# Mamba block: decays per channel group in PSUM, one scan per group, input products on GpSimd, one projection buffer

## Chip, cores, metric

The kernel runs on one NeuronCore of one Trainium2 chip. The metric is device time in microseconds (us) of one execution; less is better. Before the change the median of three runs is 3686.44 us (3685.19 to 3687.99).

## What is computed

Four graph layers in sequence over 3327 nodes with 256 features each, padded to 26 tiles of 128 nodes; each adds its result to its input and normalizes. The change touches layer 1 alone: a graph convolution, then a Mamba block whose state-space recurrence runs over the nodes in order.

```python
h = relu(adj @ x @ gcn_w + gcn_b); h = layernorm(h)
xz = h @ w_in                        # 512 channels xc, 512 channels z
u = silu(conv(xc) + conv_b)          # causal, 4 taps
dbc = u @ w_xp                       # dt (16), B (16), C (16)
dt = softplus(dbc[:, :16] @ w_dt + b_dt)
dA = exp(dt[:, :, None] * A[None])   # (L, 512, 16)
dBu = dt[:, :, None] * B[:, None, :] * u[:, :, None]
def step(hst, inp):                  # over the L nodes
    dAt, dBut, Ct = inp
    hst = dAt * hst + dBut
    return hst, hst @ Ct
_, ys = lax.scan(step, zeros, (dA, dBu, C))
y = (ys + u * D_skip) * silu(z)
return y @ w_out
```

## The kernel before

**Tiling.** Channels lie on the partitions: 512 channels are four groups (`NG`) of 128. Nodes lie along the free dimension, in eight chunks whose ends grow: 128, 256, 384 and then five times 512 nodes (`WC`). A chunk has 16 states (`DS`), so there are 128 pairs of chunk and state, and the main loop (from line 551) goes through them in order.

**One state.** `row` (L453) fetches the rows B and C of this state by a DMA that spreads them over all partitions, two states ahead, into one of three buffers. `decay` (L460) makes exp(dt*A) on ScalarE, one activation for each channel group, into one of two SBUF buffers that hold all four groups side by side, each with one extra column in front. `feed` (L471) multiplies dt*u by the row of B on VectorE into one of three buffers `db`; the extra column receives the state carried over from the chunk before (the copy `du<-carry`, L469). `scan` (L478) is one VectorE scan over all four groups at once, 4 x 513 elements, since the extra column has decay 0 and so restarts the recurrence with the carried state. ScalarE then saves the last column of each group (`carry`, L486). The product with the row of C is a VectorE multiplication in place (L568), and `add_up` (L489) adds the result, transposed on TensorE, into up to four PSUM banks `y`.

**What runs between.** `head` (L363) prepares the next chunk in eleven pieces, one with each state from the fourth on: projections to PSUM (`ps`), three VectorE multiply-adds for each group (the convolution, L379), Silu, w_xp and w_dt products, softplus in steps (L407 to L420), and dt*u (L422). `gate_input` (L427) computes z; at L580 it goes through Silu. `gate` (L496), `gated`, `residual` and `back` finish the chunk before. `pump` (L326) advances `convolve` (L254), the adjacency product of layer 1, whose TensorE work is spread between the states. Its per-tile statistics go from VectorE to three very small GpSimd instructions (L251, L252, L296) and back to ScalarE. `values` prepares layer 2.

**Order and memory.** Each engine has one in-order queue; the order within it comes from the order of the program text and a scheduler that may move independent instructions, save where the text pins them. PSUM has eight banks of 128 x 512 f32: four `y`, three `ps` (every projection takes one), one `cb` for the adjacency product.

Of the kernel before, what the change touches and what calls it, by code (L numbers as in the profile page):

```python
# [18 lines left out]
P = 128  # L19
# [5 lines left out]
WC = 512  # L25
# [18 lines left out]
def gnn_kernel(ctx: ExitStack, tc: tile.TileContext, n: int, a: dict, out: bass.AP):  # L44
# [109 lines left out]
    with tc.tile_pool(name="l1b", bufs=1) as wpool, tc.tile_pool(name="l1at", bufs=2) as l1at:  # L154
# [33 lines left out]
        with tc.tile_pool(name="l1aw", bufs=1) as cwork, tc.tile_pool(name="l1c", bufs=2) as ch, \  # L188
                tc.tile_pool(name="l1t", bufs=3) as tmp, tc.tile_pool(name="l1s", bufs=2) as work, \
                tc.tile_pool(name="l1y", bufs=1, space=PSUM) as ypsum, \  # L190
                tc.tile_pool(name="l1p", bufs=3, space=PSUM) as psum, \
                tc.tile_pool(name="l1d", bufs=1, space=DRAM) as l1d, \
                tc.tile_pool(name="l1q", bufs=1, space=PSUM) as cpsum:
            def scratch():
# [50 lines left out]
            nch = len(ends)  # L245
            starts = [0] + ends[:-1]
            hTs, us, szs, rows_of = {}, {}, {}, {}

            def power(rs, var):

# [75 lines left out]
            def pump(steps=1, tiles=0):  # L326


                nonlocal done
                while steps > 0 or done < min(tiles, nt):  # L330
                    t = next(stream, None)
                    if t is None:
                        return values()
                    done, steps = t, steps - 1
# [28 lines left out]
            def head(c):  # L363
# [7 lines left out]
                for g in range(NG + 1):  # L371
                    if g < NG:
                        nc.scalar.copy(xc[:, g, 3:3 + w], project(c, g, w))
                        nc.scalar.activation(u[:, g, :], xc[:, g, 0:w], AF.Identity, scale=conv_w[:, g, 0:1],
                                             bias=conv_b[:, g:g + 1])
                    if g:
                        ug = u[:, g - 1, :]
                        for k in range(1, 4):
                            nc.vector.scalar_tensor_tensor(ug, xc[:, g - 1, k:k + w], conv_w[:, g - 1, k:k + 1], ug,  # L379
                                                           op0=ALU.mult, op1=ALU.add)  # L380
                    if g < NG:
                        yield None
                nc.gpsimd.tensor_copy(last, xc[:, :, w:w + 3])
                yield None
                nc.scalar.activation(u, u, AF.Silu)
                ps = psum.tile([P, WC], F32, name="ps")
                for g in range(NG):
                    nc.tensor.matmul(ps[:w_sp.shape[2], :w], w_sp[:, g, :], u[:, g, :],
# [10 lines left out]
                for g0 in range(0, NG, 2):  # L399
# [7 lines left out]
                        nc.scalar.activation(v[:, g, :], ps[:, :w], AF.Identity, bias=b_dt[:, g:g + 1])  # L407
                        nc.scalar.activation(e[:, g, :], ps[:, :w], AF.Abs, bias=b_dt[:, g:g + 1])
                    yield None
                nc.scalar.activation(e, e, AF.Exp, scale=-1.0)  # L410
                e1 = scratch()[:, :, :w]
                nc.scalar.activation(e1, e, AF.Identity, bias=1.0)
                yield None
                nc.vector.scalar_tensor_tensor(e, e1, 1.0, e, op0=ALU.subtract, op1=ALU.subtract)
                yield None
                nc.scalar.activation(e1, e1, AF.Ln)
                yield None
                nc.vector.tensor_sub(e1, e1, e)
                dt = ch.tile([P, NG, WC], F32, name="dt", bufs=1)[:, :, :w]
                nc.vector.scalar_tensor_tensor(dt, v, 0.0, e1, op0=ALU.max, op1=ALU.add)  # L420
                du = by_group(ch.tile([P, NG * (1 + WC)], F32, name="du", bufs=1), w)
                nc.vector.tensor_mul(du[:, :, 1:], dt, u)  # L422
                for g in range(NG):
                    nc.scalar.mul(u[:, g, :], u[:, g, :], d_skip[:, g:g + 1])
                yield c, dt, du
# [1 line left out]
            def gate_input(c, i):  # L427
# [5 lines left out]
                for k in range(2):  # L433
# [5 lines left out]

            dAs, dbs = ([cwork.tile([P, NG * (1 + WC)], F32, name=f"{x}{i}") for i in range(m)]
                        for x, m in (("dA", 2), ("db", 3)))

            def by_group(t, w):
                return t[:, :NG * (1 + w)].rearrange("p (g w) -> p g w", g=NG)


            lines = [cwork.tile([P, 2, 1 + WC], F32, name=f"row{i}") for i in range(3)]
            for r in lines:  # L450
                nc.vector.memset(r[:, 0, 0:1], 1.0)

            def row(c, s):  # L453

                w = us[c].shape[2]
                r = lines[(c * DS + s) % 3][:, :, :1 + w]
                nc.sync.dma_start(r[:, :, 1:], rows_of[c][None, :, s, :].to_broadcast([P, 2, w]))
                return r

            def decay(x, s):  # L460

                c, dt, du = x
                w = dt.shape[2]
                dA = by_group(dAs[s % 2], w)
                if s < 2 and (c == 0 or w != ends[c - 1] - starts[c - 1]):
                    nc.gpsimd.memset(dA[:, :, 0:1], 0.0)
                for g in range(NG):
                    nc.scalar.activation(dA[:, g, 1:], dt[:, g, :], AF.Exp, scale=A[:, g, s:s + 1])  # L468
                nc.scalar.copy(du[:, :, 0], carry[:, s, :])  # L469

            def feed(x, s, B):  # L471

                du = x[2]
                w = du.shape[2] - 1
                tc.keep_in_program_order(nc.vector.tensor_mul(  # L475
                    by_group(dbs[(x[0] * DS + s) % 3], w), du, B[:, 0:1, :].to_broadcast([P, NG, 1 + w])))

            def scan(x, s):  # L478

                w = x[1].shape[2]  # L480
                h = dbs[(x[0] * DS + s) % 3]
                m = NG * (1 + w)
                nc.vector.tensor_tensor_scan(h[:, :m], dAs[s % 2][:, :m], h[:, :m],  # L483
                                             initial=0.0, op0=ALU.mult, op1=ALU.add)
                h = by_group(h, w)
                nc.scalar.copy(carry[:, s, :], h[:, :, w])  # L486
                return h[:, :, 1:]

            def add_up(ys, h, first=False, last=False):  # L489

# [26 lines left out]
            def back(c):  # L517

                m = szs[c].shape[1]
                mv = small.tile([P, WC // P, 2], F32, name="mvc")  # L520
                ahead = gated(c, 0)
                for i in range(m):
                    gt, ahead = ahead, gated(c, i + 1) if i + 1 < m else None
                    residual(c, i, gt)
                    stats(mv[:, i, :], X[:, starts[c] // P + i, :])
                rs = small.tile([P, WC // P], F32, name="rsc")
                power(rs[:, :m], mv[:, :m, 1])
# [11 lines left out]
                yield  # L539

            pump(tiles=ends[0] // P)
            x = None
            for i, x in enumerate(head(0)):
                if i % 2:
                    pump()
            states = [(c, s) for c in range(nch) for s in range(DS)]
            rows = [row(*states[0]), row(*states[1])]
            decay(x, 0)
            feed(x, 0, rows[0])
            ys = ahead = None  # L550
            for c in range(nch):
                w = us[c].shape[2]
                for s in range(DS):
                    if s + 1 < DS:
                        nxt = (x, s + 1)
                    else:
                        nxt = (y, 0) if c + 1 < nch else None
                    k = c * DS + s + 2
                    if k < len(states):
                        rows.append(row(*states[k]))  # L560
                    if nxt:
                        decay(*nxt)
                    h = scan(x, s)
                    if s == 0 and c:
                        gate(c - 1, ys)
                    if nxt:
                        feed(*nxt, rows[1])
                    nc.vector.tensor_mul(h, h, rows.pop(0)[:, 1:2, 1:].to_broadcast([P, NG, w]))  # L568
                    if s == 0:
                        ys = [ypsum.tile([P, DI], F32, name=f"y{i}") for i in range(w // P)]  # L570
                        add_up(ys, us[c], first=True)
                    add_up(ys, h, last=(s == DS - 1))
                    if s == 0 and c:
                        tail = back(c - 1)
                    if s in (0, 4) and c:
                        next(tail)
                    if 2 <= s < 2 + w // P:
                        gate_input(c, s - 2)
                    if s == 8:
                        nc.scalar.activation(szs[c], szs[c], AF.Silu)  # L580
                    if c or s % 4 < 3:
                        pump()
                    if DS - 13 <= s < DS - 1 and c + 1 < nch:
                        if s == DS - 13:
                            pump(steps=0, tiles=ends[c + 1] // P)
                            ahead = head(c + 1)
                        y = next(ahead)
                if c + 1 < nch:
                    x = y
            gate(nch - 1, ys)  # L590

            m = us[nch - 1].shape[2] // P
            ahead = gated(nch - 1, 0)
            for i in range(m):
                it = starts[nch - 1] // P + i
                gt, ahead = ahead, gated(nch - 1, i + 1) if i + 1 < m else None
                residual(nch - 1, i, gt)
                mv = small.tile([P, 2], F32, name="mv")
                stats(mv, X[:, it, :])
                rs, nb = (small.tile([P, 1], F32, name=x) for x in ("rs", "nb"))  # L600
# [815 lines left out]
```

## Time and profile before

One execution was profiled: its own time is 3689.87 us, the profile's span 3688.1 us, the median of the runs 3686.44 us.

| stretch of the span (us) | what | length | TensorE busy | VectorE busy | ScalarE busy | GpSimd busy | granted clock |
|---|---|---|---|---|---|---|---|
| 0 to 394 | layer 0 and the start of layer 1 | 394 | 383.60 | 73.10 | 41.20 | 3.21 | 1.00 |
| 394 to 475 | chunk of 128 | 81 | 75.98 | 52.18 | 57.94 | 8.80 | 0.95 |
| 475 to 585 | chunk of 256 | 110 | 95.68 | 91.34 | 67.06 | 35.16 | 0.92 |
| 585 to 715 | chunk of 384 | 130 | 109.88 | 126.66 | 78.65 | 41.15 | 0.92 |
| 1541 to 1566 | end of layer 1 | 25 | 19.64 | 7.62 | 8.36 | 4.25 | 0.87 |
| 1566 to 3688 | layers 2 and 3 | 2122 | 2021.12 | 1432.73 | 1040.44 | 374.51 | 0.98 |

How to read it: busy is the time in which an engine worked on an instruction; the granted clock is TensorE's, as a share of full speed. The boundaries are the starts of each chunk's first scan. The four full chunks with a successor (715 to 1392) and the last one (to 1541) are shown with the prediction.

### The profile page before, as it was taken

To read this page: it belongs to the slowest core of one execution; us is meant where nothing else is said; L and a number is where in the kernel's file an instruction comes from. 1 tells how busy PE (TensorE), PEld (TensorE's weight loads), DVE (VectorE), ACT (ScalarE), POOL (GpSimd) and SP (SyncE) were. 2 spreads that over 40 slices of the span, in tenths; PEclk is the share of its full clock that TensorE was granted. 3 is DMA by queue.
4 is the path that set the end of the run, shared out by engine and by line. 5 is a ranking of instruction groups with operands and counts; after the bars stand their busy time and mean duration, and the time that the engine had idled before them with its cause. 6 is when DMAs were issued, how large, how long until landed. Compare 5 with 4: busy or idle time off the path is not lost. (4 is left out here: it accounts for less than half of the span.)

```text
span 3688.1 us, 42873 instructions
## 1 busy us (share of the span) xinstructions
PE 3277.3 (89%) x15583; PEld 2588.6 (70%) x15583; DVE 2577.8 (70%) x5207; ACT 1711.3 (46%) x2736; POOL 671.5 (18%) x850
## 2 busy tenths in 40 slices
PE   9999988887778656599989999999999899999996
PEld 7888766656556444488867777777777577777775
DVE  1111588999999999777754544544541999999996
ACT  1000665554546555211123333333334888888883
POOL 0000032343334100011110000000000233333332
PEclk9999999988888778699999999999999999999998
DMA  7443343332323121144422212112112222222220
GB/s 246 140 132 101 103 112 108 101 96 85 95 82 92 46 58 48 35 156 152 147 92 62 56 52 65 56 53 65 55 54 64 61 59 67 67 67 64 64 62 22
DMA packets 151993, 308.00 MB, mean 84 GB/s; under 512 B 19858, under 2 KB 73266, under 8 KB 151634
## 3 DMA queue, kind: packets, MB, share of 16 engines
q1 hardware_dynamic: 151762, 305.06, 27.8%
q8 instruction: 127, 2.08, 0.2%
q14 instruction: 104, 0.85, 0.1%
HBM read 294.36 MB, written 10.65 MB: 83 GB/s over the span
## 5 line engine op out<-in xcount | busy, mean ns | idle before, releaser
L483 DVE TENSOR_TENSOR_SCAN db<-dA,db 128x2052 f32<-128x2052 f32 (+3 forms) x128 | 464.1, 3626 | 0.7
L493 PE MATMUL y<-ident,db 128*128 128x128 f32 x1664 | 265.6, 323 | 142.6 <-DVE db L568 142.5
L493 PEld LDWEIGHTS y<-ident,db 128*128 128x128 f32 x1664 | 239.2, 170 | 186.9 <-DVE db L568 163.9
L892 PE MATMUL acc<-X,wt 128*128 128x256 f32 x1352 | 345.2, 392 | 10.5 <-ACT wt L890 10.2
L859 PE MATMUL acc<-F,at 128*128 128x256 f32 x1352 | 352.9, 386 | 1.0 <-ACT q L633 0.6
L892 PE MATMUL acc<-G,wt 128*128 128x256 f32 x1352 | 335.9, 391 | 5.8 <-ACT wt L823 5.5
L266 PE MATMUL cb<-F,at 128*128 128x256 f32 x1352 | 323.8, 392 | 9.4 <-ACT hn L287 8.1
L892 PEld LDWEIGHTS acc<-X,wt 128*128 128x128 f32 x1352 | 243.7, 190 | 105.7 <-issue 41.3
L116 PE MATMUL acc<-xa,at 128*128 128x257 f32 x1352 | 308.8, 381 | 5.9 <-DMA at<-in_adjT 5.8
L859 PE MATMUL acc<-X,at 128*128 128x256 f32 x1352 | 308.4, 381 | 0.0
L768 PE MATMUL acc<-F,at 128*128 128x257 f32 x1352 | 304.0, 381 | 0.7 <-ACT r L741 0.7
L904 DVE MAX8 cand<-e 128x8 f32<-128x128 f32 x676 | 142.3, 281 | 227.9 <-ACT e L845 216.3
L266 PEld LDWEIGHTS cb<-F,at 128*128 128x128 f32 x1352 | 260.4, 198 | 56.8 <-ACT hn L287 12.7
L468 ACT ACTIVATE dA<-dt,A_log 128x512 f32<-128x512 f32 (+3 forms) x512 | 294.3, 636 | 9.8 <-DVE dt L420 9.5
L892 PEld LDWEIGHTS acc<-G,wt 128*128 128x128 f32 x1352 | 250.1, 193 | 65.1 <-ACT wt L823 34.9
L859 PEld LDWEIGHTS acc<-F,at 128*128 128x128 f32 x1352 | 237.2, 190 | 75.0 <-issue 50.2
L116 PEld LDWEIGHTS acc<-xa,at 128*128 128x128 f32 x1352 | 255.3, 191 | 43.3 <-issue 6.6
L859 PEld LDWEIGHTS acc<-X,at 128*128 128x128 f32 x1352 | 252.8, 191 | 39.9 <-issue 7.8
L768 PEld LDWEIGHTS acc<-F,at 128*128 128x128 f32 x1352 | 253.7, 191 | 36.6 <-issue 1.0
L475 DVE TENSOR_TENSOR db<-du,row 128x2052 f32<-128x2052 f32 (+3 forms) x128 | 241.0, 1883 | 28.7 <-PE y L493 17.8
L568 DVE TENSOR_TENSOR db<-db,row 128x2048 f32<-128x2048 f32 (+3 forms) x128 | 241.5, 1887 | 26.6 <-ACT carry L486 26.6
L890 ACT COPY wt<-tp 128x512 f32<-128x512 f32 (+1 forms) x182 | 93.7, 557 | 311.0 <-PE tp L888 310.6
(307 smaller groups left out, 5382.0 us busy)
## 6 DMA issues: line engine op xcount, KB each, us to landing
at<-in_adjT SPq DMA_DIRECT2D x102, 832.0 KB, 4.5
at<-in_adjT SPq DMA_DIRECT2D x260, 320.0 KB, 3.0
row<-bc SPq DMA_DIRECT2D x80, 512.0 KB, 4.9
at<-in_adjT SPq DMA_DIRECT2D x52, 576.0 KB, 3.9
at<-in_adjT SPq DMA_DIRECT2D x26, 512.0 KB, 3.7
row<-bc SPq DMA_DIRECT2D x16, 384.0 KB, 5.0
row<-bc SPq DMA_DIRECT2D x16, 256.0 KB, 4.7
xt<-in_xT SPq DMA_DIRECT2D x26, 128.0 KB, 4.1
```

What stands on the lines that cost most here:

```text
L116: nc.tensor.matmul(acc, at[:, j, :], rhs[:, j0 + j, :], start=(j0 + j == 0), stop=(j0 + j == nt - 1))
L266: nc.tensor.matmul(acc, at[:, j % JC, :], X0[:, j, :], start=(j == 0), stop=(j == nt - 1))
L468: nc.scalar.activation(dA[:, g, 1:], dt[:, g, :], AF.Exp, scale=A[:, g, s:s + 1])
L475: tc.keep_in_program_order(nc.vector.tensor_mul(by_group(dbs[(x[0] * DS + s) % 3], w), du, B[:, 0:1, :].to_broadcast([P, NG, 1 + w])))
L483: nc.vector.tensor_tensor_scan(h[:, :m], dAs[s % 2][:, :m], h[:, :m], initial=0.0, op0=ALU.mult, op1=ALU.add)
L493: nc.tensor.matmul(y[:, g * P:(g + 1) * P], h[:, g, i * P:(i + 1) * P], ident, is_transpose=True, start=(first and g == 0), stop=(last and ...
L568: nc.vector.tensor_mul(h, h, rows.pop(0)[:, 1:2, 1:].to_broadcast([P, NG, w]))
L768: nc.tensor.matmul(acc, at[:, j, :], F[:, j0 + j, :], start=(j0 + j == 0), stop=(j0 + j == nt - 1))
L859: nc.tensor.matmul(acc, at[:, j, :], rhs[:, j0 + j, :], start=(j0 + j == 0), stop=(j0 + j == nt - 1))
L890: copy(wt[:, :m, :], pt[:, :m, :])
L892: nc.tensor.matmul(acc, wt[:, j, :], rhs[:, j0 + j, :], start=(j0 + j == 0), stop=(j0 + j == nt - 1))
L904: nc.vector.max(cand[:, s * 8:(s + 1) * 8], z[:, s * SEG:(s + 1) * SEG])
```

## The change

- **Decays in PSUM, one group each.** `decay(k, g)` writes exp(dt*A) of one group to a PSUM bank of its own, of which there are two (pool `l1a`). The two big SBUF buffers, the extra columns and the copy `du<-carry` go.
- **One scan per group.** Four scans of 512 instead of one of 2052; the carried state is the scan's `initial` operand, one value for each partition.
- **Input products on GpSimd.** `feed(k)` becomes a GpSimd multiplication of the same size, issued two states ahead, into two buffers `h` in place of three `db`. It waits for the product and the carry copy of state k-2, which read the same buffer.
- **Products** with the row of C go to two buffers of their own (`hc`).
- **One `ps` buffer** for all projections, where there were three; the banks are now four `y`, one `ps`, two `dA`, one `cb`.
- **Order.** `chained` pins the order of the scans, products and `head`'s VectorE instructions; `decaying` that of the decays, both Silu and Ln on ScalarE. `head`'s pieces are placed after the scans and ahead of the product; its Exp and the addition of 1 are issued by group. `gated` is no longer issued one tile ahead of `residual`. Silu of z moves from state 8 to state 7. `dt` gets a second buffer.

```diff
-                tc.tile_pool(name="l1p", bufs=3, space=PSUM) as psum, \
+                tc.tile_pool(name="l1p", bufs=1, space=PSUM) as psum, \
+                tc.tile_pool(name="l1a", bufs=2, space=PSUM) as apsum, \
...
+            def decaying(*x, **k):
+                with tc.issue_after(decays[-1].ins) if decays else nullcontext():
+                    decays.append(nc.scalar.activation(*x, **k))
+
+            def chained(op, *x, **k):
+                with tc.issue_after(chain[-1].ins) if chain else nullcontext():
+                    chain.append(op(*x, **k))
...
-                nc.scalar.activation(e, e, AF.Exp, scale=-1.0)
-                nc.scalar.activation(e1, e, AF.Identity, bias=1.0)
+                for g in range(NG):
+                    nc.scalar.activation(e[:, g, :], e[:, g, :], AF.Exp, scale=-1.0)
+                    nc.scalar.activation(e1[:, g, :], e[:, g, :], AF.Identity, bias=1.0)
...
-                for g in range(NG):
-                    nc.scalar.activation(dA[:, g, 1:], dt[:, g, :], AF.Exp, scale=A[:, g, s:s + 1])
-                nc.scalar.copy(du[:, :, 0], carry[:, s, :])
+                dA = apsum.tile([P, WC], F32, name="dA")[:, :w]
+                decaying(dA, dt[:, g, :], AF.Exp, scale=A[:, g, states[k][1]:states[k][1] + 1])
+                return dA
...
-                tc.keep_in_program_order(nc.vector.tensor_mul(
-                    by_group(dbs[(x[0] * DS + s) % 3], w), du, B[:, 0:1, :].to_broadcast([P, NG, 1 + w])))
+                nc.gpsimd.tensor_tensor(hs[k % 2][:, :, :w], du, rows[k][:, 0:1, :].to_broadcast([P, NG, w]), op=ALU.mult)
...
-                nc.vector.tensor_tensor_scan(h[:, :m], dAs[s % 2][:, :m], h[:, :m],
-                                             initial=0.0, op0=ALU.mult, op1=ALU.add)
+                h = hs[k % 2][:, g, :dA.shape[1]]
+                chained(nc.vector.tensor_tensor_scan, h, dA, h, initial=carry[:, s, g:g + 1] if c else 0.0,
+                        op0=ALU.mult, op1=ALU.add)
...
+            rows = {k: row(k) for k in range(2)}
+            for k in range(2):
+                feed(k)
+            dAs = [decay(0, g) for g in range(2)]
...
+                for g in range(NG):
+                    scan(k, g, dAs.pop(0))
+                    if g < 2:
+                        dAs.append(decay(k, g + 2))
+                    elif k + 1 < len(states):
+                        dAs.append(decay(k + 1, g - 2))
+                with tc.high_priority():
+                    nc.scalar.copy(carry[:, s, :], hs[k % 2][:, :, w - 1])
+                if s == 7:
+                    decaying(szs[c], szs[c], AF.Silu)
+                if DS - 13 <= s < DS - 1 and c + 1 < nch:
...
+                    xs[c + 1] = next(ahead)
+                h = product(k)
+                if k + 2 < len(states):
+                    feed(k + 2)
```

## The prediction

> **What bounds the kernel now.** The page first. Its chain of waits is no help: it ends after one instruction (ACT h L1138). So I read the costliest groups, cut the span at the first scan of each chunk, and asked for busy times in these stretches. Columns: length, then busy us (and instructions) of PE, PEld, DVE, ACT, POOL, then granted clock, DMA share, GB/s.
>
> ```profile
> 715.00:882.00 167.00, 134.45 (x640) 102.96 (x638) 162.45 (x85) 88.48 (x164) 64.70 (x19) 0.89 0.34 99
> 882.00:1056.00 174.00, 132.46 (x616) 102.55 (x616) 163.81 (x89) 88.58 (x165) 62.38 (x19) 0.85 0.31 89
> 1056.00:1228.00 172.00, 123.80 (x564) 94.96 (x564) 163.77 (x89) 88.53 (x165) 54.63 (x19) 0.84 0.28 76
> 1228.00:1392.00 164.00, 100.79 (x444) 76.62 (x445) 159.70 (x80) 90.41 (x192) 15.03 (x7) 0.76 0.19 51
> 1392.00:1541.00 149.00, 79.88 (x380) 65.02 (x379) 144.45 (x64) 61.61 (x143) 7.68 (x4) 0.75 0.19 48
> ```
>
> In the five full chunks VectorE is busy for 94 to 97%; nothing else is above 81%. The stage is bound by VectorE. The groups by shape say by what (count, busy us, mean ns):
>
> ```profile
> L483 DVE TENSOR_TENSOR_SCAN db<-dA,db 128x2052 f32<-128x2052 f32 x80 | 354.0, 4426 | 0.0
> L568 DVE TENSOR_TENSOR db<-db,row 128x2048 f32<-128x2048 f32 x80 | 182.9, 2287 | 18.9 <-ACT carry L486 18.9
> L475 DVE TENSOR_TENSOR db<-du,row 128x2052 f32<-128x2052 f32 x80 | 182.4, 2281 | 0.0
> ...
> L483 DVE TENSOR_TENSOR_SCAN db<-dA,db 128x516 f32<-128x516 f32 x6 | 7.4, 1229 | 0.1
> ```
>
> A state costs scan, feed, product. In the timeline each starts 0.09 us before its predecessor ends, so 4.34 + 2.19 + 2.19 = 8.72 us, times 16 = 139.5 a chunk. `head`, gates and statistics add 12 x 0.655 (L379, 744 ns) + 4 x 2.19 (L414 to L422) + 4 x 0.59 (L498) + 4 tiles x 1.15 (L515, L84, L85 from 412, 416 to 420, 177 ns) = 23.6. Sum 163.1; the four chunks up to 1392 last 169.3 on average. So about 6 us of a chunk are waits.
>
> **Feeds leave VectorE.** -2.19 us a state. What they cost on GpSimd: the trace has an addition of two 128x256 inputs at 726 ns (L1129) and one of 128x1 at 190 (L1014), so 2.10 ns an element; 2048 elements make 4.49 us (estimate). The Trainium skill, "GPSIMD Engine Reference", section "Performance versus the Vector engine", speaks against such a move, with 4497 ns against 2293; that price and the row's slope agree. What decides is the port. In the same skill "Perfetto Trace Analysis", section "Optimizing Scalar/DVE Operations", warns that moving work between these two engines might not help, since they share an SBUF read port. The trace shows both halves of that:
>
> ```profile
> 714.82 0.66 DVE L498 TENSOR_TENSOR sz<-y,sz 128x512 f32<-128x512 f32 x1
> ...
> 714.99 0.22 POOL L251 TENSOR_SCALAR rs<-mv 128x1 f32<-128x1 f32 x1 [8.54 <-DVE mv L85]
> ...
> 715.30 0.57 POOL L252 TENSOR_TENSOR rs<-rs,mhalf 128x1 f32<-128x1 f32 x1
> ...
> 715.40 4.42 DVE L483 TENSOR_TENSOR_SCAN db<-dA,db 128x2052 f32<-128x2052 f32 x1
> ...
> 715.97 3.92 POOL L296 TENSOR_SCALAR nb<-mv,rs 128x1 f32<-128x1 f32 x1
> ...
> 2927.22 0.73 POOL L873 TENSOR_TENSOR t<-t,s 128x256 f32<-128x256 f32 x1
> 2927.26 0.71 DVE L978 TENSOR_TENSOR c<-c,tot 128x1 f32<-128x1 f32 x1
> ```
>
> L296, one element wide and 0.26 us long in idle stretches, takes 3.92 us and ends with the scan, which has two SBUF inputs. Conversely L978 (146 ns at its shortest) lasts until GpSimd is done. But beside L498, whose one input is PSUM, L251 and L252 take their usual 0.22 and 0.57. Moving the decays to PSUM turns the scan into an instruction of L498's kind. So I take it that a feed runs beside four scans and excludes only the products and `head`'s SBUF pairs. By the skill's warning taken for every VectorE instruction, a state would be 11.9 instead of 7.2 us; that is rival C.
>
> **One scan per group, from PSUM.** The two scan rows give (4426 - 1229)/(2052 - 516) = 2.08 ns an element and 155 ns fixed: 1.22 us at 512. A PSUM input costs nothing more in the nearest rows (L498, 679 ns; L568 at 512, 686). The new `initial` pointer: L379 with its pointer takes 744 against 686, so +0.06. 1.28 us, 1.19 if it overlaps its predecessor fully; I take 1.25, so 5.0 a state, +0.66. Bounds: 1.13 (no pointer cost, full overlap) and 1.40 (a PSUM access dearer than L498 shows).
>
> **Does the feed fit?** Feed(k+2) starts when product(k) is done and has to end before product(k+1) wants the port: 4.49 plus two handovers of 0.08 (L85 ends at 714.91, L251 starts at 714.99) = 4.65 against 5.0 of scans. It fits with 0.35 to spare. The rows come two states ahead and land in 4.9 us (row<-bc), well inside two states. The carry copy (0.2) hides behind the product; the old wait of products for it (18.9 us over 80) goes, since the product no longer writes in place.
>
> **Small GpSimd work** is in the same queue: three instructions for each tile of statistics, 0.23 + 0.57 + 0.26 and gaps = 1.2 us, and four for each chunk's end. A feed behind them starts late and makes the next product late by about 0.8: 5 such places a full chunk, 4 us.
>
> **Decays on ScalarE.** 64 x 0.719 a chunk as before. With two banks a decay may begin when the scan two before it ends, and 0.72 + handovers is below 1.25: hidden, with 0.4 us to spare. What ScalarE has besides, 88.5 - 46.0 - 3.1 (the `du` copies that go) - 2.6 (two of six table loads go, as the two Silu stand together) = 37 us a chunk or 2.3 a state, fits under the product (2.19) and that slack, save two blocks. In the new instruction order table load, Silu, a 0.38 copy, Silu, table load stand between two decays: 1.28 + 1.91 + 0.38 + 1.91 + 1.28 = 6.8, and the next decay 0.72, against two scans in store (2.5): 5 us of waiting. Table load, Ln, table load: 4.5 + 0.7 - 2.5 = 3 us (rounded up). Before, a whole state of decays lay in store and both were hidden.
>
> **One `ps` bank.** Some 30 uses a chunk; each occupies it for matmul and copy, 1.2 + 0.6 us (L434, L436): 54 of 150 us, so it need not bind. TensorE can wait for it in its queue, where the `y` transposes and the adjacency matmuls stand behind. TensorE was busy for 134 us with 167 to spend, and its matmuls shorten little when the clock rises. I charge 3 us in each of the three chunks where it still has adjacency work. At the end of layer 1 (1541 to 1566), where three banks overlapped tiles, and at the start: +6 together.
>
> **The sum.** Full chunk: 64 x 1.25 + 16 x 2.19 + 23.6 = 138.6; waits 8 (ScalarE) + 4 (GpSimd) + 2 (rest of today's 6) = 152.6 against 169.3: -16.7, times 4 = -67. Last chunk: 80 + 35 + 2.4 + 3 = 120.4, wait 4: 124 against 149, -25. Chunk of 384: 64 x 0.98 + 16 x 1.66 + 16.7 + 6 + waits 13 (8 + 3 + 2) = 125 against 130, -5. Chunk of 256: VectorE would need 80, but TensorE is busy for 96: 106 against 110, -4. Chunk of 128: TensorE 76 of 81, 0. With +9 and +6: -86. The profiled execution, 3689.9, would become 3604; on the median, 3686.4, **3600 us**. Its own range, from scans at 1.13 to 1.40 (5 x 64 x 0.12 = 38 down, 48 up): 3560 to 3648.
>
> **Rivals.**
> A. TensorE takes over. For: 110 busy of 130 and 96 of 110 in the small chunks, a single `ps` bank, and a queue in which the transposes wait for products. Against: it had 33 us idle in each full chunk. If chunks 3 to 5 can't go below 160, the gain there is 3 x 11 and the small chunks give nothing: -33 - 17 - 25 + 6, 3617; with copies stuck behind decays twice as often, about 3645.
> B. ScalarE's queue is exposed. If all 37 us of its other work stand between scans, chunks reach 138.6 + 37 = 176, +6 each, the last 139, -10: about +20 with the end, 3705. Against: the order puts most of it beside products. It decides where more than 30 of the 37 are exposed.
> C. The feed excludes the scans, too. The place: scan with one SBUF tensor and an SBUF pointer, which no row of the trace shows. Then a state is 2.19 + 5.0 + 4.65 = 11.8, the chunk 189 + 24 + 8 = 221, +52 x 4, the last +45: about +270 with the small chunks, 3955. It is slower than before as soon as over 1.5 of the 4.65 us are not beside scans. Against: L251 and L252 beside L498.
> That the change does not do what it says: the instruction order shows four PSUM scans and one GpSimd feed a state, so no.
>
> **How the numbers follow.** Forecast 0.60; A, with dearer PSUM scans, 0.24; B 0.09; C 0.07. The range takes the forecast's own range, reaches down by 10 for waits I have overcharged, and up through A, 3550 to 3680. A measurement here tells about 0.2% (7 us). Faster: the first two, 0.84. Within: half of B's lower edge, 0.04. Slower: the rest of B, and C, 0.12.
>
> **What would show it.** Right: no VectorE feeds, scans of 1.2 to 1.3 us, feeds of 4.5 us that end before the product starts, full chunks of 150 to 156, and VectorE waits named ScalarE at Silu and Ln, 8 us a chunk. Wrong: feeds of 7 us and more or that end with a product (GpSimd shut out), scans waiting for a decay in every state (B), `y` transposes or `ps` copies ahead of most waits (A), scans longer than 1.4 us.

## The result and the profile after

| | median, us | runs | from, to |
|---|---|---|---|
| before | 3685.82 | 4 | 3683.99, 3687.99 |
| after | 3619.64 | 4 | 3617.05, 3620.64 |

The ratio is 0.9819, 95% interval 0.9802 to 0.9836: the kernel became 66 us faster. Forecast was 3600 with a range of 3550 to 3680. The profiled execution after took 3620.6 us, its span is 3618.6.

The stretches of the profile, cut as before at the first scan of each chunk (length, then busy us and instructions of PE, PEld, DVE, ACT and POOL, granted clock, DMA share, GB/s). These are the five full chunks and the end of layer 1:

```profile
722.60:874.30 151.70, 132.67 (x632) 99.48 (x630) 135.87 (x117) 86.89 (x150) 87.46 (x34) 0.92 0.37 108
874.30:1023.30 149.00, 127.65 (x616) 95.67 (x616) 136.77 (x121) 87.96 (x152) 88.67 (x35) 0.93 0.36 103
1023.30:1171.80 148.50, 118.72 (x576) 88.80 (x576) 136.96 (x121) 87.85 (x152) 88.63 (x35) 0.91 0.31 89
1171.80:1330.10 158.30, 110.12 (x448) 72.96 (x448) 135.48 (x113) 93.63 (x183) 77.08 (x23) 0.78 0.20 54
1330.10:1459.20 129.10, 78.77 (x390) 61.04 (x390) 117.89 (x97) 64.33 (x129) 71.44 (x19) 0.83 0.22 57
1459.20:1496.00 36.80, 26.63 (x88) 17.59 (x88) 6.92 (x18) 8.62 (x21) 4.22 (x12) 0.69 0.00 0
```

VectorE is still the busiest engine of every full chunk, but at 86 to 92% in place of 94 to 97%: its work fell by more than the chunk did. The last row shows the other side of the change: the end of layer 1 takes 36.8 us, where it took 25, and its clock is 0.69, where it was 0.87.

| stretch | before, us | after, us | forecast, us |
|---|---|---|---|
| first scan starts at | 394.5 | 398.5 | see end of layer 1 |
| chunk of 128 | 81 | 88.8 | 81 |
| chunk of 256 | 110 | 101.7 | 106 |
| chunk of 384 | 130 | 133.6 | 125 |
| four full chunks, mean | 169.9 | 151.9 | 152.6, and 3 more in three of them |
| last chunk | 146 | 129.1 | 124 |
| end of layer 1 | 25 | 36.8 | +6, the start with it |

Before the change the last chunk's first scan starts at 1395.1 us; the cut at 1392 in the tables of before lies 3 us too early. Here these 3 us are counted with the chunk ahead of it. The full chunks gave 72 us and the last one 17. The small chunks took back 3 in sum, the end of layer 1 and its start 16. Layers 2 and 3 are as long as before (2122 us before, 3618.6 - 1496.0 = 2122.6 after).

VectorE's groups by shape between 430 and 1500 us (count, busy us, mean ns, idle time ahead of them and its releaser):

```profile
L257 DVE TENSOR_TENSOR_SCAN h<-dA,carry,h 128x512 f32<-128x512 f32 x320 | 391.9, 1267 | 31.7 <-ACT dA L253 31.5
L257 DVE TENSOR_TENSOR hc<-h,row 128x2048 f32<-128x2048 f32 x80 | 183.1, 2289 | 3.3
...
L257 DVE SCALAR_TENSOR_TENSOR u<-t,conv_w,u 128x512 f32<-128x512 f32 x60 | 45.1, 752 | 35.9 <-ACT u L384 34.5
```

Line 257 is the helper `chained`, line 253 `decaying`, so the tiles tell the groups apart. No feed is left here; it stands in GpSimd's groups of layer 1 (from 380 to 1500 us):

```profile
L476 POOL TENSOR_TENSOR h<-du,row 128x2048 f32<-128x2048 f32 x80 | 362.3, 4529 | 297.9 <-DVE hc L257 240.6 <-issue 36.8 <-ACT F L363 14.3
```

The scans take 1.27 us each, the feeds 4.53. A state in which nothing is late reads as follows in the timeline (start, duration, in brackets the idle time before and its releaser):

```profile
821.26 4.84 DVE L257 TENSOR_TENSOR_SCAN h<-dA,carry,h 128x512 f32<-128x512 f32 x4
...
821.48 4.53 POOL L476 TENSOR_TENSOR h<-du,row 128x2048 f32<-128x2048 f32 x1 [3.43 <-DVE hc L257]
...
826.20 2.29 DVE L257 TENSOR_TENSOR hc<-h,row 128x2048 f32<-128x2048 f32 x1
...
828.41 3.63 DVE L257 TENSOR_TENSOR_SCAN h<-dA,carry,h 128x512 f32<-128x512 f32 x3
```

The feed lies wholly beside the four scans: it ends at 826.01, the scans at 826.10, and the product starts at 826.20. The state is 828.41 - 821.26 = 7.15 us, where it was 8.72. VectorE's waits in layer 1 after the change (390 to 1500 us: total, times, longest):

```profile
DVE h L257 <- ACT dA L253: 59.5, 50, 5.7
DVE u L257 <- ACT u L384: 46.6, 26, 4.1
DVE bnst L84 <- ACT hn L297: 46.3, 10, 17.3
DVE X L519 <- PE ps L518: 16.6, 4, 7.2
```

The first row is the one that was forecast: scans that wait for decays. The second was not: the multiply-adds of `head`'s convolution wait for ScalarE's first tap (L384). The third is layer-norm statistics in VectorE's queue, which wait for ScalarE's copies of TensorE's adjacency columns; 19.0 of its 46.3 us are in the chunk of 128, where TensorE is busy for 76.85 of 88.8 us. The fourth is the end of layer 1.

### The profile page after: what moved, and what is told of

The parts are those of the page before. It is cut to its first block, busy times and chain, and to the rows that moved or that the text cites. A ratio compares the mean times of both kernels' runs of the same rounds, so it can differ in the third digit from the quotient of the medians.

```text
span 3618.6 us, 43460 instructions
## 1 busy us (share of the span) xinstructions
PE 3287.3 (91%) x15583; PEld 2564.1 (71%) x15583; DVE 2414.3 (67%) x5460; ACT 1707.9 (47%) x2642; POOL 939.9 (26%) x970
## 5 line engine op out<-in xcount | busy, mean ns | idle before, releaser
L476 POOL TENSOR_TENSOR h<-du,row 128x2048 f32<-128x2048 f32 (+3 forms) x128 | 475.3, 3714 | 432.9 <-DVE hc L257 301.9
L257 DVE TENSOR_TENSOR_SCAN h<-dA,carry,h 128x512 f32<-128x512 f32 (+2 forms) x448 | 496.8, 1153 | 47.2 <-ACT dA L253 46.9
L253 ACT ACTIVATE dA<-dt,A_log 128x512 f32<-128x512 f32 (+3 forms) x512 | 308.0, 609 | 241.4 <-DVE h L257 240.2
L497 PE MATMUL y<-ident,hc 128*128 128x128 f32 x1664 | 256.3, 309 | 76.8 <-DVE hc L257 76.5
L497 PEld LDWEIGHTS y<-ident,hc 128*128 128x128 f32 x1664 | 224.5, 161 | 133.1 <-DVE hc L257 100.1
L257 DVE TENSOR_TENSOR hc<-h,row 128x2048 f32<-128x2048 f32 (+3 forms) x128 | 245.4, 1917 | 5.7 <-PE y L497 0.5
```

The lines of the kernel that those rows point to most:

```text
L253: decays.append(nc.scalar.activation(*x, **k))
L257: chain.append(op(*x, **k))
L476: nc.gpsimd.tensor_tensor(hs[k % 2][:, :, :w], du, rows[k][:, 0:1, :].to_broadcast([P, NG, w]), op=ALU.mult)
L497: nc.tensor.matmul(y[:, g * P:(g + 1) * P], h[:, g, i * P:(i + 1) * P], ident, is_transpose=True, start=(first and g == 0), stop=(last and ...
```

## Experiments

The theory after the result: the feed is free because the scan has only one SBUF tensor left; what is missing against the forecast is lost to the one `ps` bank, above all at the end of layer 1, and in the chunks to ScalarE's order. Each run has its ratio to the kernel before. Medians from different chips differ by a few us (that of the kernel before was 3681 to 3689), so small differences are taken from ratios or from a stretch of the trace.

### The feed back on VectorE

```diff
-                nc.gpsimd.tensor_tensor(hs[k % 2][:, :, :w], du, rows[k][:, 0:1, :].to_broadcast([P, NG, w]), op=ALU.mult)
+                chained(nc.vector.tensor_mul, hs[k % 2][:, :, :w], du, rows[k][:, 0:1, :].to_broadcast([P, NG, w]))
```

> The changed kernel with one part undone: the input products go back to VectorE, right behind the product of the state two before. Theory (the gain is the feeds leaving VectorE, the four smaller scans by themselves cost): each state gets 2.19 us longer at 512 nodes, 1.66 at 384, 1.13 at 256, 0.6 at 128, together about 230 us, of which waits may absorb 30: 3800 to 3850 us, slower than the kernel before. Rival (the gain comes from the new order, the smaller decays and the carry that no longer blocks the product): close to 3620.

Measured: 3774.8 us, ratio 1.0257 (1.0235 to 1.0279). Its timeline:

```profile
1007.51 4.80 DVE L257 TENSOR_TENSOR_SCAN h<-dA,carry,h 128x512 f32<-128x512 f32 x4
1012.41 2.29 DVE L257 TENSOR_TENSOR hc<-h,row 128x2048 f32<-128x2048 f32 x1
1014.79 2.29 DVE L257 TENSOR_TENSOR h<-du,row 128x2048 f32<-128x2048 f32 x1
1017.00 3.63 DVE L257 TENSOR_TENSOR_SCAN h<-dA,carry,h 128x512 f32<-128x512 f32 x3
```

The state is 9.49 us, 2.34 longer, which is 37 us a chunk. Three full chunks of this run are 178, 176 and 184 us, 27 more than after's on average: the other 10 were waits, for VectorE's waits on L384 are gone and those of the scans fall from 59.5 to 33.3 us. So the rest of the change without its feed loses 2.6% against the kernel before, as expected in sign, and moving the feed is worth 155 us by the medians, 161 by the ratios. The size was expected at 180 to 230: in the longer state more waits for ScalarE went than the 30 us that the expectation allowed for.

### The decays in SBUF

```diff
-                tc.tile_pool(name="l1a", bufs=2, space=PSUM) as apsum, \
+                tc.tile_pool(name="l1a", bufs=2) as apsum, \
...
-            hs, prods = ([cwork.tile([P, NG, WC], F32, name=f"{x}{i}") for i in range(2)] for x in ("h", "hc"))
+            hs, prods = ([cwork.tile([P, NG, WC], F32, name=f"{x}{i}") for i in range(m)] for x, m in (("h", 2), ("hc", 1)))
...
-                g = prods[k % 2][:, :, :w]
+                g = prods[0][:, :, :w]
```

Order, tile shapes and instructions are after's; the scan reads two SBUF tensors again. The second `hc` gave the room.

> The changed kernel with the two decay buffers in SBUF instead of PSUM, so that a scan has two SBUF inputs; to find the room, the products have one buffer instead of two. Theory (a VectorE instruction with two SBUF inputs shuts a GpSimd one out for its whole length): feeds run only while VectorE stands still, a full state is 2.3 + 4.8 + 4.7 = 11.8 us instead of 7.1, +490 us over all chunks less absorbed waits: 4000 to 4100. Rival (the port is shared in part): 3700 to 3900, feeds stretched beside the scans. Second rival (PSUM only saves room): 3620.

Measured: 3996.2 us, ratio 1.0859 (1.0835 to 1.0882), 377 us above after and just below the range of the theory. VectorE's and GpSimd's groups of this run:

```profile
L257 DVE TENSOR_TENSOR_SCAN h<-dA,carry,h 128x512 f32<-128x512 f32 x320 | 706.7, 2254 | 11.2 <-ACT dA L253 8.9 <-ACT col L361 2.3
```
```profile
L476 POOL TENSOR_TENSOR h<-du,row 128x2048 f32<-128x2048 f32 x80 | 413.8, 5173 | 463.0 <-DVE hc L257 404.1 <-issue 42.8 <-ACT col L361 6.9
```

The mean scan is 987 ns longer and the mean feed 644. The timeline shows how:

```profile
1257.78 1.27 DVE L257 TENSOR_TENSOR_SCAN h<-dA,carry,h 128x512 f32<-128x512 f32 x1
1258.00 5.39 POOL L476 TENSOR_TENSOR h<-du,row 128x2048 f32<-128x2048 f32 x1 [9.80 <-DVE hc L257]
...
1259.40 0.42 DVE L519 TENSOR_TENSOR X<-F,ps 128x256 f32<-128x256 f32 x1 [0.34 <-PE ps L518]
1259.74 4.73 DVE L257 TENSOR_TENSOR_SCAN h<-dA,carry,h 128x512 f32<-128x512 f32 x1
```

The feed begins inside a scan and ends 0.86 us late (5.39 against 4.53): the scan of 1.27 us holds it until 1259.05. The next scan is issued at 1259.74, while the feed runs until 1263.39, and ends at 1264.47, 1.08 us after the feed: it worked behind the feed and is recorded with 4.73. Scans of this run with no feed beside them take 1.24 to 1.28 us (three from 1264 to 1271), so a decay in SBUF is no slower to read. Between them L519, which reads one SBUF tensor and a PSUM tile, takes its usual 0.42 us in the middle of the same feed. So two SBUF tensors exclude GpSimd, one and PSUM don't. The trace agrees with the Trainium skill ("SBUF — State Buffer", section "SBUF: two separate sides"): of a VectorE instruction with two SBUF inputs and a GpSimd one that reads SBUF, whichever starts first has the shared port pair for its whole length. One buffer `hc` costs something here too (products waited 23 us for `y` transposes), so 377 is not the port alone.

### The kernel before with one `ps` bank

```diff
-                tc.tile_pool(name="l1p", bufs=3, space=PSUM) as psum, \
+                tc.tile_pool(name="l1p", bufs=1, space=PSUM) as psum, \
...
-                ahead = gated(c, 0)
                 for i in range(m):
-                    gt, ahead = ahead, gated(c, i + 1) if i + 1 < m else None
-                    residual(c, i, gt)
+                    residual(c, i, gated(c, i))
```

The last loop of the layer is changed in the same way.

> The kernel before with one change: one PSUM bank for projections instead of three, and the transposes at a chunk's end no longer one tile ahead. It prices the single bank by itself. Theory: it costs mostly at the end of layer 1, where the tiles' round trips then stand in a row (11 to 13 us), and little in the chunks, whose bound is VectorE: +10 to +25 us, 3696 to 3711. Rival (the single bank holds up TensorE and ScalarE in every chunk): +40 and more.

Measured: 3693.5 us, ratio 1.0036 (1.0022 to 1.0051). The window from the end of its last product to layer 2:

```profile
1536.90:1574.75 37.85, 27.16 (x88) 18.25 (x88) 6.91 (x17) 8.64 (x22) 4.28 (x12) 0.69 0.00 0
```

This end is 13 us longer than before's 25 us, at the same clock of 0.69 as after the change. The bank has a price at the start, too: the first scan starts at 401.5 us (394.5 before) and the second chunk at 486.5 (475.4 before). From there to the end of the last product this run takes 1050 us, before 1066. So with VectorE as the bound one bank cost these seven chunks nothing; why they became shorter is not shown, and the edit also no longer issues the transposes one tile ahead.

### Idle banks for the end of the layer

No scan is left at the end of the layer, so the two banks of the decays are free. Added to the change:

```diff
+            spare = []
+            def bank():
+                return apsum.tile([P, WC], F32, name="dA") if spare else psum.tile([P, WC], F32, name="ps")
...
-                pt = psum.tile([P, NG, P], F32, name="ps")
+                pt = bank().rearrange("p (g w) -> p g w", g=NG)
...
-                po = psum.tile([P, WC], F32, name="ps")[:, :D]
+                po = bank()[:, :D]
...
+            spare.append(1)
+            ahead = gated(nch - 1, 0)
             for i in range(m):
-                residual(nch - 1, i, gated(nch - 1, i))
+                gt, ahead = ahead, gated(nch - 1, i + 1) if i + 1 < m else None
+                residual(nch - 1, i, gt)
```

> The changed kernel with one addition: after the last scan the two decay banks, then idle, take the chunk-end transposes and output projections, again one tile ahead. Theory (the end of layer 1 grew from 24 to 37 us because every round trip takes the single bank): -8 to -12 us, 3607 to 3612. Rival (TensorE's lower granted clock there, or the later start of layer 2, is the cause): no change, 3616 to 3623.

Measured: 3608.5 us (3607.0 to 3611.8), ratio 0.9807 (0.9793 to 0.9822). The window of the end:

```profile
1460.90:1484.10 23.20, 18.55 (x88) 14.13 (x88) 6.86 (x19) 8.32 (x22) 4.24 (x12) 0.94 0.00 0
```

36.8 us became 23.2. The same 88 matmuls are busy for 18.55 us instead of 26.63: 8 of the 13.6 us are matmuls that run slower (0.69 against 0.94 of the clock), only the rest is waiting itself. The two banks, with the transposes one tile ahead, brought the clock back. By the ratio alone the gain would not be told from none, since the two intervals overlap; the profiled spans differ by 12.0 us.

### The projections of `head` earlier in the text

Theory: ScalarE's copies for the convolution come late because `head`'s pieces stand after the scans. The first half of each piece (projection, copy, first tap) was moved ahead of the state's scans, the multiply-adds stayed.

```diff
+                if DS - 13 <= s < DS - 12 + NG and c + 1 < nch:
...
+                    next(ahead)
                 for g in range(NG):
                     scan(k, g, dAs.pop(0))
```

> The changed kernel with each channel group's projection and its two ScalarE copies issued ahead of the state's scans instead of behind them; the multiply-adds on VectorE stay where they are, one state after. Theory (the multiply-adds, pinned between scans and product, wait for ScalarE copies that stand behind the decays, 5 to 9 us a chunk in six chunks): most of these waits go, -20 to -35 us, 3585 to 3600. Rival (the copies then delay the decays by as much, so ScalarE is short of time, not of order): within 8 us of 3620.

Measured: 3616.9 us, ratio 0.9812 (0.9789 to 0.9834), no change; the multiply-adds still wait 48 us. The instruction order tells why this run settles nothing on its own: in both traces, from 776 to 800 us, ScalarE has three decays, copy, carry copy, decay, tap in a state. The scheduler had put the copies back behind the decays. Together with the idle banks the same edit added nothing either:

> The early projections and the spare banks at the end of layer 1 together. If both theories hold, their gains add up, since they lie in different stretches: 3575 to 3592. If only the bank counts: 3608 to 3612.

Measured: 3610.8 us, ratio 0.9794 (0.9774 to 0.9813), what the idle banks gave alone.

### The multiply-adds free to move

```diff
-                            chained(nc.vector.scalar_tensor_tensor, ug, xc[:, g - 1, k:k + w], conv_w[:, g - 1, k:k + 1], ug,
+                            nc.vector.scalar_tensor_tensor(ug, xc[:, g - 1, k:k + w], conv_w[:, g - 1, k:k + 1], ug,
```

> The changed kernel with the multiply-adds of the convolution no longer pinned in VectorE's order; the scheduler then puts many of them between scans. Theory (their waits for ScalarE come from where they stand, and between scans they would shut GpSimd's feed out): waits move rather than go, feeds end later and products or scans wait for them: 3605 to 3640. Rival (the pin is the whole of the cost): -20 to -35 us.

Measured: 3638.2 us, ratio 0.9869 (0.9844 to 0.9893), slower than after. The waits of VectorE in this run:

```profile
DVE h L257 <- ACT dA L253: 58.1, 52, 5.5
...
DVE u L389 <- ACT u L384: 18.8, 11, 5.8
DVE hc L257 <- PE y L497: 18.6, 6, 10.0
```

Without the pin the multiply-adds wait 18.8 us instead of 46.6, and a new wait of 18.6 stands ahead of the products. That is 10 us less in these two rows, and yet the run is slower. The multiply-adds themselves show why (700 to 1500 us):

```profile
L389 DVE SCALAR_TENSOR_TENSOR u<-t,conv_w,u 128x512 f32<-128x512 f32 x48 | 67.8, 1413 | 10.4 <-ACT u L384 10.1
```

Their mean is 1413 ns, pinned it was 752: 32 us more in all. They read two SBUF tensors, and the scheduler put some of them between scans, beside a feed. One is issued at 787.39 us and recorded with 3.82; the feed beside it ends at 790.66, 0.55 ahead of it. That is the pattern of the scans with decays in SBUF once more. The feeds stay at 4567 ns. So the pin of `chained` costs waits and is still worth having. Of the 18.3 us between the two spans 10.8 had come up when the last product started; 6.6 lie in layers 2 and 3.

### ScalarE's copies pinned

On top of the idle banks, copy and tap of a convolution group are put into the pinned order of the decays, behind the last decay of a state. They can then run while VectorE does multiply-adds and product (in after ScalarE was idle for 4.68 us there).

```diff
-                        nc.scalar.copy(xc[:, g, 3:3 + w], project(c, g, w))
-                        nc.scalar.activation(u[:, g, :], xc[:, g, 0:w], AF.Identity, scale=conv_w[:, g, 0:1],
-                                             bias=conv_b[:, g:g + 1])
+                        decaying(xc[:, g, 3:3 + w], project(c, g, w), AF.Copy)
+                        decaying(u[:, g, :], xc[:, g, 0:w], AF.Identity, scale=conv_w[:, g, 0:1],
+                                 bias=conv_b[:, g:g + 1])
```

> On top of e4_tail_banks (3608): the two ScalarE operations of a convolution group (copy from the bank, first tap) are put into the decays' own order, behind the last decay of a state. They then run in the 4.7 us in which ScalarE stands idle before the next state's scans, and no longer behind three decays that wait for scans. Theory (the multiply-adds wait because of ScalarE's order, not its amount of work): waits of the multiply-adds fall from 47 us to under 15, 3575 to 3595. Rival (the projection itself comes late, behind the one bank): the decays now wait for TensorE in the copies' place, and the time stays at 3603 to 3620.

Measured: 3594.9 us (3591.4 to 3598.9), ratio 0.9739 (0.9718 to 0.9761), the fastest of all and clear of the interval of the idle banks alone. Its waits, VectorE's and then ScalarE's:

```profile
DVE h L257 <- ACT dA L253: 96.9, 58, 5.6
DVE bnst L84 <- ACT hn L297: 41.2, 9, 15.8
```
```profile
ACT t L253 <- PE ps L369: 61.6, 26, 4.1
```

Both theories were half right. The multiply-adds wait for ScalarE no more, so order was a cause. But the decays, now behind the copies, are waited for 97 us instead of 58, since the copies wait for their projections. The timeline of this run shows what those wait for:

```profile
748.24 1.88 PE L445 MATMUL ps<-w_in,hT 128*128 128x512 f32 x4
...
749.96 4.06 PE L276 MATMUL cb<-F,at 128*128 128x256 f32 x18
...
751.12 0.58 ACT L447 COPY sz<-ps 128x512 f32<-128x512 f32 x1
...
753.86 1.88 PE L369 MATMUL ps<-hT,w_in 128*128 128x512 f32 x4
...
755.77 0.60 ACT L253 ACTIVATE t<-ps 128x512 f32<-128x512 f32 x1 [4.08 <-PE ps L369]
...
758.32 2.46 DVE L257 TENSOR_TENSOR_SCAN h<-dA,carry,h 128x512 f32<-128x512 f32 x2 [1.18 <-ACT dA L253]
```

The gate's projection (L445) holds the one bank from 748.24 until its copy ends at 751.70; in TensorE's queue 18 adjacency matmuls then stand ahead of the convolution's projection, which ends at 755.74. In this trace the last product of layer 1 starts at 1436.2 us, 22.5 earlier than with the idle banks alone (1458.6). Of these, 21 us lie in the three small chunks (304.7 against 326.0); the first three full chunks gave 6, and the fourth took 6 back. The spans differ by 13.3 only: the end of layer 1 is 1.7 longer, and layers 2 and 3 took 7.5 us more (2130.0 against 2122.5; all traces here lie between 2122 and 2130). Why they vary is not shown.

### One place earlier, and the projections first

Two variants: the pinned copies directly behind the decay of a state's last group, with the multiply-adds in the same state, on the idle banks; and the pinned copies as above with the projections at high priority.

```diff
+                    if g == 2 and DS - 13 <= s < DS - 12 + NG and c + 1 < nch:
...
+                        next(ahead)
                     if g < 2:
                         dAs.append(decay(k, g + 2))
```

> As e8_conv_pinned, but the two operations stand one place earlier, directly behind the decay of a state's last group, and the multiply-adds come in the same state. Theory: 3575 to 3595, with waits of the multiply-adds under 15 us. Rival (the projection comes late behind the one bank): scans wait for decays that stand behind the copy, 3603 to 3630.

Measured: 3606.5 us, ratio 0.9771 (0.9747 to 0.9796), within the rival's range; scans wait 97.7 us for decays, once for 9.7.

```diff
-                        decaying(xc[:, g, 3:3 + w], project(c, g, w), AF.Copy)
+                        with tc.high_priority():
+                            pg = project(c, g, w)
+                        decaying(xc[:, g, 3:3 + w], pg, AF.Copy)
```

> On top of e8_conv_pinned (3595): the convolution's projections are put ahead of other work in TensorE's order, so that the copies no longer wait for them (ScalarE waited 62 us for these projections there). If the rest of the wait is TensorE's order: 3570 to 3588, and ScalarE's wait for the projections falls below 30 us. If it is the one bank, which the gate's projections hold in the same states, nothing falls: 3590 to 3605.

Measured: 3608.5 us, ratio 0.9787 (0.9766 to 0.9808), above both ranges. ScalarE's wait for these projections falls from 61.6 to 41.0 us, not below 30 as expected if TensorE's order were the rest of the wait; scans still wait 100 us for decays, and the last product starts at 1458.0, as with the idle banks alone. Shifting work in one queue moved the wait along. A second bank for the convolution's projections was not tried, since the kernel has its eight banks in use while scans run; whether the bank or TensorE's order holds the rest stays open.

## Why the prediction was right

- **The port.** Taken from L251 and L252 beside L498: right, and shown by the decays in SBUF. Rival C's mechanism is real; it just doesn't hold for a scan that reads PSUM. The `initial` pointer in SBUF does not bring the lock.
- **The feed.** Forecast 4.49 us, measured 4.53. The Trainium skill's price in "GPSIMD Engine Reference", section "Performance versus the Vector engine" (4497 ns), agrees; as a reason against the move it doesn't hold here, where the cheaper engine is the bound and the feed on VectorE makes the kernel 155 us slower.
- **The scan.** Forecast 1.25 between 1.13 and 1.40. Alone it takes 1.27; a chain of four takes 4.80 to 4.84, so 1.20 each. PSUM and pointer cost what the nearest rows said.
- **The fit.** 0.35 us to spare was 0.1: the scans came out 0.2 shorter than taken, and the feed starts 0.2 after them. It held, and with slightly faster scans the feed would be the bound of a state. In the chunk of 128 feeds that start late met products: two of these took 1.80 and 1.13 us (at 462.00 and 465.55) in place of 0.69, and ended 0.55 us after the feed beside them.
- **Small GpSimd work.** 4 us a chunk was charged; scans waited for a feed twice, 3.6 us in the whole of layer 1, both times in the chunk of 128. In the other chunks it was hidden.
- **ScalarE's two blocks.** 8 us a chunk was charged. In the three chunks from 722.6 to 1171.8 the scans waited 3 to 6 us a chunk for decays; the Silu block cost 1.5 us (2.46 us of scans at 808.55 after a wait of 1.54) and Ln 0.8, because most of each block ran beside multiply-adds and a product. In their place came the convolution's taps at 5 to 8 us a chunk, which the sum did not have. Waits of 11.5 to 16 us (length less busy) against 14 forecast are therefore a right total from partly wrong terms, which is luck in part. In the chunk from 1171.8 waits reached 22.8: 10.0 for decays, 5.5 for taps, and one of 6.4 for softplus.
- **TensorE's surcharge.** 3 us in each of three chunks: not needed; they average (151.7 + 149.0 + 148.5) / 3 = 149.7. With one bank and TensorE busy for up to 87% of the stretch, VectorE still set the pace. So rival A failed in the full chunks. The reason given, that matmuls shorten little with the clock, holds in these chunks: the 616 of the second took 132.46 us at 0.85 and 127.65 at 0.93. It does not hold at the end of layer 1.
- **The end of layer 1: the step that was too small.** "At the end of layer 1 (1541 to 1566), where three banks overlapped tiles, and at the start: +6 together" measured +12 and +4. The waiting was counted, the clock not: the same 88 matmuls took 26.63 us at 0.69, where they took 19.64 at 0.87, so 7 of the 12 us are slower matmuls. The kernel before with one bank shows the same (27.16 at 0.69), and with the idle banks they take 18.55. At the start, one bank alone delayed the first scan by 7.0 us.
- **The small chunks.** Forecast 0, -4 and -5; measured +8, -8 and +4. In the chunk of 128 statistics stood in VectorE's queue ahead of scans for 17.3 us, waiting for an adjacency column of TensorE; this is rival A's place. The kernel before with one bank comes to nearly the same times without any of the other edits: its second and third chunks start at 486.5 and 587.6 us (after the change 487.3 and 589.0; before it, with three banks, 475.4 and 585.0). So the loss in the first small chunk and the gain in the second go with the single bank; by what path is not shown. In the chunk of 384 waits were 24.4 us against 13 forecast: 9.4 for taps, 7.9 for decays, 6.0 for statistics.
- **The last chunk.** Forecast 124, measured 129.1: waits for decays of 10.0 against 4. One of 5.7 is at its Silu, where the gate's copy ahead of it had waited 3.2 us for its projection, which had waited 1.7 for the one bank; another 3.3 are decays behind copies of `values`, which waited for the bank as well.

In the stretches of the trace the sum was -86 us by the forecast and -70 by measurement. Against their forecast lengths the full chunks came out 12 us shorter in all, surcharge included; the end and the start 10 longer, the last chunk 5, the small chunks 12. The early cut at 1392 moves 3 us from one term to another and does not touch the sum.

## What to carry to other kernels

Before moving VectorE work to GpSimd, count the SBUF tensors of what VectorE will do at that time: with one of its two inputs in PSUM the two engines ran side by side, with both in SBUF the same move cost more than it saved. When PSUM banks are taken from one use for another, look at the stretches where the other use is asleep, and lend them back there. And where waits are to be removed by moving instructions, see in the trace that the order really changed, and watch for the same wait behind the next engine.

## What was not expected of the hardware

- A locked instruction's record begins when it is issued, not when it can work: 4.73 us for a scan of 1.27, 3.82 for a multiply-add of 0.75. A row of such means looks like a slow instruction, and only the other engine's timeline tells.
- The granted clock fell with waits that are short. At the end of layer 1 after the change no gap between matmul groups was over 1.4 us once the last `y` transposes had begun, and the clock was 0.69. It fell within the stretch, as the same eight matmuls show:

  ```profile
  1467.62 1.99 PE L518 MATMUL ps<-w_out,gt 128*128 128x256 f32 x8 [0.73 <-ACT gt L510]
  ...
  1474.88 2.98 PE L518 MATMUL ps<-w_out,gt 128*128 128x256 f32 x8 [0.67 <-ACT gt L510]
  ...
  1484.40 3.78 PE L518 MATMUL ps<-w_out,gt 128*128 128x256 f32 x8 [0.67 <-ACT gt L510]
  ```

  With the idle banks one gap was 1.49 us long and the clock 0.94, so the longest gap did not decide here. TensorE stood idle for 28% of the stretch in the one case and for 20% in the other. The Trainium skill ("TensorE: Matmul & The Clock Gate", section "A second HAM failure mode: psum-queue depth-cycling") describes, for another kernel, frequent short idling between matmul groups as a cause of a clock that falls and rises again; the three windows of 88 matmuls here, 26.63 and 27.16 us at 0.69 against 18.55 at 0.94, agree with it.
